# A graph-network layer on one Trainium2 core: x loaded ahead of most convolution taps, and the first message moved between the filter steps

## The chip, the cores and the metric

The kernel runs on one core of one Trainium2 chip. The core has TensorE (PE, matrix products), VectorE (DVE), ScalarE (ACT), GpSimd (POOL), SyncE (SP, used here for DMA issue alone) and 16 DMA engines that all queues share. The metric is the device time of one execution, in microseconds, lower being better. The kernel before takes 1842.6 us (median of 3 runs, 1842.21 to 1846.51). A difference of 0.3%, about 5.5 us, is what a measurement of this kernel can tell from none.

## The reference

64 graphs of 256 nodes with 256 channels. A layernorm and a relu give h; a graph layer of h is added to x.

```python
h = jnp.maximum(_layernorm(x, axis=-1), 0.0)
# the layer, with x standing for h, and mask for adj
xc = jnp.transpose(x, (0, 2, 1))
h = relu(_bn(_conv1d(xc, conv1_w, 0), bn1...))          # 1 tap
h = _bn(_conv1d(h, conv2_w, 8), bn2...)                 # 17 taps along the nodes
x_conv = jnp.transpose(jax.nn.relu(h + xc), (0, 2, 1))
s = x @ w_se.T + b_se                                   # 3 numbers a node
sq = jnp.sum(s * s, axis=-1)
dist = sq[:, :, None] + sq[:, None, :] - 2.0 * jnp.einsum('bnd,bmd->bnm', s, s)
A = jnp.exp(-dist) * mask
msg = jax.nn.relu(x @ w_msg.T + b_msg)
x_nmp = jnp.einsum('bnm,bmd->bnd', A, msg)
x_in = jnp.concatenate([x_conv, x_nmp], axis=-1)
gi = x_in @ w_ih.T + b_ih
gh = x @ w_hh.T + b_hh                                  # then the gates of a GRU cell
```

All in float32.

## The kernel before

The 64 graphs are worked in pairs (32 pairs, numbered i from 0), and eight graphs, four pairs, make a batch b. The convolution with 17 taps is done as a fast transform along the nodes: VectorE transforms conv1's output (`split_steps`, `fft.odd`, `fft.even`), TensorE multiplies each of 16 frequency bins with transformed weights (`products`, which reads tiles `wb`), and VectorE transforms back. The transformed weights are made by the kernel itself, once, at the start. That start is what the change rearranges; the 1740 us after it are the same in both kernels but for what had been done earlier.

**The filter steps.** The taps (`c2_wT`, 256 input channels x 17 taps x 256 output channels, 4.46 MB) are laid out as 19 groups g of 7 input channels: 7 x 17 = 119 rows of a tile `taps`, for each of two chunks dc of 128 input channels. A step `filters(m, g, eng)` multiplies the group with a constant matrix `points[m]` (three of them, m = 0, 1, 2, for bins 0 to 5, 6 to 11, 12 to 15), copies the result from PSUM to a tile `fo` on ScalarE (L716; six buffers, used in turn), and stores it to a DRAM tensor `filt[m]` by the queue `eng` (L717). There are 57 steps. The first 18 take the groups 0 to 5 with all three m, the other 39 go through the groups 6 to 18 for m = 0, then for m = 1, then for m = 2. Stores go to GpSimd's queue and SyncE's in turn. `load_kind` (L728) loads the tiles `wb` from `filt`, nine of them before the last 17 steps.

The taps are loaded in parts (`load_taps`): `PARTS[0]` is groups 0 to 2, `PARTS[1]` groups 3 to 5, `PARTS[2]` groups 6 to 17, each for chunk 0 and chunk 1, first the 112 rows that split evenly; `load_last_taps` loads the seven rows left over, for all groups, and `load_last_group` group 18. Chunk 0 comes by SyncE's queue, chunk 1 by ScalarE's.

**Beside the filter steps** the first four pairs are normalised and pass conv1, in program order between the steps. `norm(i)`: VectorE takes statistics of X (L559 to L564), GpSimd raises the variance to the power of -0.5 (`rstd`, L565), VectorE scales X (L571). `transpose_h(i)`: TensorE transposes X into PSUM (L521), VectorE (pair 0) or ScalarE copies it with a relu to `hT`. `conv1(i)`: TensorE multiplies with `w_c1`, VectorE or ScalarE applies bn1 to give `h1`; `split_steps(i)` on VectorE follows. X of pairs 0 and 1 lies in tiles x, of pair 2 in tile Sv, of pair 3 in tile PT. `columns("bn1")` is a small TensorE transpose of bn1's four vectors, and is the first instruction of TensorE.

**Order.** [...]each engine works its instructions in the order of the program, and a waiting instruction holds up what is behind it on its engine, or on its DMA queue. A small planner (`Pace`) places VectorE's transform steps among the other work by estimated times. Each DMA raises a semaphore when it lands. Those of SyncE and ScalarE share eight in turn, those of GpSimd have eight of their own, so the issue of a DMA waits until the eighth before it has landed.

After the steps come the batches: `message(i)` (messages and s of a pair), `embed(i)` (a transpose of s-based rows `z`), `affinity(i)` (distances, exp, times adj), and `products`, `aggregate` and `gates` among them.

```python
    filter_steps(2)
    transpose_h(0)
    norm(1)
    for j in range(PB):
        ...
        conv1(j)
        ...
        run(split_steps(j))
        filter_steps((4, 4, 2, 2)[j])
    forward()
    filter_steps(len(steps) - (NG - FIRST) - 4)
    ...
    filter_steps(len(steps))
```

Of the kernel before, what the change touches and what calls it, by code (L numbers as in the profile page):

```python
# [13 lines left out]
FP = mybir.dt.float32  # L14
U16 = mybir.dt.uint16
AF = mybir.ActivationFunctionType
# [285 lines left out]
def kernel(  # L302
# [26 lines left out]
    nc = tc.nc  # L329
# [112 lines left out]
    make_identity(nc, ident)  # L442
    neg_half = const.tile([P, G * MC], FP)
    nc.gpsimd.memset(neg_half, -0.5)

# [8 lines left out]
    def load_taps(dc, a, b, eng):  # L456
        v = c2_wT[dc * P + a * KG:dc * P + b * KG].rearrange("(g k) t o -> (k t) g o", k=KG)
        eng.dma_start(out=taps[:MAIN, a:b, dc, :], in_=v[:MAIN])
# [31 lines left out]
            eng.dma_start(out=t[a:a + n[j]], in_=v.rearrange("(k p) -> k p", p=P))  # L490
        ROWS[name] = t, n

    load_vectors("bn2", bn2 + [ih_b, hh_b], nc.gpsimd)
    load_points(0, nc.scalar)
    for dc, eng in ((0, nc.sync), (1, nc.scalar)):
        load_taps(dc, *PARTS[0], eng)
        load_last_taps(dc, eng)
    load_x(0)
    load_vectors("bn1", bn1, nc.scalar)
    w_c1 = const.tile([P, DC, D], FP)  # L500
    nc.scalar.dma_start(out=w_c1, in_=c1_wT.rearrange("(k p) o -> p k o", p=P))
    for n in range(1, len(PASSES)):
        load_points(n, nc.scalar)
    load_taps(0, *PARTS[1], nc.sync)
    load_x(1)
    load_taps(1, *PARTS[1], nc.scalar)
    load_taps(0, *PARTS[2], nc.sync)
    load_taps(1, *PARTS[2], nc.scalar)
    load_last_group(0, nc.sync)
    load_last_group(1, nc.scalar)  # L510
    load_x(2)
    load_x(3)

    pace = Pace()

# [71 lines left out]
        run(b)  # L587

    norm(0)
    def fold_bn(params, name, factor=1.0):  # L590
        g, b, m, v = params
        scale = const.tile([P, DC], FP, name=f"{name}_scale")
        shift = const.tile([P, DC], FP, name=f"{name}_shift")
        nc.vector.tensor_scalar(scale, v, BN_EPS, None, ALU.add)
        nc.gpsimd.tensor_tensor(scale, scale, neg_half[:, :DC], ALU.pow)
        nc.vector.tensor_mul(scale, scale, g)
        nc.vector.tensor_mul(shift, m, scale)
        nc.vector.tensor_sub(shift, b, shift)
        if factor != 1.0:
            nc.vector.tensor_scalar(scale, scale, factor, None, ALU.mult)  # L600
        return scale, shift

    bn1 = columns("bn1")
    nc.scalar.activation(const.tile([P, 1], FP, name="unused"), neg_half[:, :1], AF.Relu)
    s1, h1_shift = fold_bn(bn1, "bn1")


# [334 lines left out]
    steps = deque((m, g) for g in range(FIRST) for m in range(len(PASSES)))  # L942
    steps.extend((m, g) for m in range(len(PASSES)) for g in range(FIRST, NG))

    def filter_steps(n):
        for k in range(n):
            filters(*steps.popleft(), nc.gpsimd if len(steps) % 2 else nc.sync)

    filter_steps(2)
    transpose_h(0)  # L950
    norm(1)
    for j in range(PB):
        if j > 0:
            transpose_h(j)
        if 0 < j < PB - 1:
            norm(j + 1)
        if j == 2:

            w_msg = const.tile([P, DC, D + SE], FP)
            nc.gpsimd.dma_start(out=w_msg[:, :, D:], in_=se_wT.rearrange("(k p) s -> p k s", p=P))  # L960
            b_msg = const.tile([P, D + SE], FP)
            for t, v in ((b_msg[:, :D], msg_b), (b_msg[:, D:], se_b)):
                nc.gpsimd.dma_start(out=t, in_=bass.AP(tensor=v.tensor, offset=v.offset, ap=[[0, P], [1, v.shape[0]]]))
            nc.sync.dma_start(out=w_msg[:, :, :D], in_=msg_wT.rearrange("(k p) o -> p k o", p=P))
            load_adj(0, nc.sync)
        conv1(j)
        if j == 2:
            *bn2, b_ih, b_hh = columns("bn2")
            s2, h2_shift = fold_bn(bn2, "bn2", 1.0 / L)
            b_rz = const.tile([P, 2 * DC], FP)  # L970
            nc.vector.tensor_add(b_rz, b_ih[:, :2 * DC], b_hh[:, :2 * DC])
            nc.vector.tensor_scalar(b_rz, b_rz, 0.5, None, ALU.mult)
        run(split_steps(j))
        filter_steps((4, 4, 2, 2)[j])
    forward()
    filter_steps(len(steps) - (NG - FIRST) - 4)
    for n in range(3):
        for kind in range(3):
            load_kind(0, n, kind)
# [6 lines left out]
    for b in range(NB):  # L986
        i = b * PB
        nxt = i + PB
        message(i)
        pace.flush(odd)  # L990
        products(b, 0)
        embed(i)
        products(b, 1)
        pace.add(fft.branch_back(Yv, T, 0))
        affinity(i)
        if b > 0:
            load_adj(i + 1)
        products(b, 2)
        if b > 0:
            finish(i - 1)  # L1000
        else:
            transpose_a(i)
        products(b, 3)
        pace.flush(even)
        if b == 0:
            norm(nxt)
        else:
            run(norm_steps(nxt + 1)[0])
        pace.add(fft.branch_back(Yv, T, 2))
        pace.add(fft.odd_back(Yv, T))  # L1010
        aggregate(i)
        if b > 0:
            join_adj(i + 1)
        else:
            nc.gpsimd.dma_start(out=w_hh, in_=hh_wT.rearrange("(k p) o -> p k o", p=P))
            nc.gpsimd.dma_start(out=w_ih, in_=ih_wT.rearrange("(k p) o -> p k o", p=P))
        products(b, 4)
        message(i + 1)
        products(b, 5, lambda i=i: embed(i + 1))
        pace.add(mix(fft.q_back(Yu, T), fft.odd_factors(Yv)))  # L1020
        if b == 0:
            pace.add(norm_steps(nxt + 1)[0], normed[1])
        affinity(i + 1)
        if b > 0:
            load_adj(i + 2)
            join_h(nxt)
        products(b, 6)
        if b == 0:
            transpose_a(i + 1)
            transpose_h(nxt)  # L1030
        products(b, 7)
        pace.add(mix(fft.p_back(Yu, T), fft.q_factors(Yu)), scaled)

        def join(j):
            pace.add(fft.join(Yu, Yv, T, slice(2 * G * j, 2 * G * (j + 1))))
            pace.add([(W, lambda o=o: residual(i + j, o)) for o in range(DC)], joined[j])
        join(0)
        pace.add(norm_steps(nxt + 2)[0], normed[2])
        join(1)
        if b == 0:  # L1040
            turn_adj(3)
            keep_adj(3)
        aggregate(i + 1)
        if b > 0:
            join_adj(i + 2)
        message(i + 2)
        pace.flush(normed[1])
        turn_h(nxt + 1)

        def wait():  # L1050
            pace.flush(scaled)
            affinity(i + 2, True)
            conv1(nxt)
            pace.add(split_steps(nxt), halved)
            join(2)
            pace.flush(joined[0])
        gates(i, 0, wait, lambda i=i: embed(i + 2))
        if b == 0:
            transpose_a(i + 2)
            load_y(0)  # L1060
        load_adj(i + 3)
        sort_h(nxt + 1)
        turn_adj(nxt)
        keep_adj(nxt)

        def early():
            join_h(nxt + 1)
            pace.flush(normed[2])
            turn_h(nxt + 2)
        gates(i, 1, None, early)  # L1070
        pace.flush(halved)
        conv1(nxt + 1)
        join(3)
        pace.add(split_steps(nxt + 1), halved)
        pace.add(norm_steps(nxt + 3)[0], normed[3])
        aggregate(i + 2)
        join_adj(i + 3)
        pace.flush(joined[1])
        sort_h(nxt + 2)
        turn_adj(nxt + 1)  # L1080
        keep_adj(nxt + 1)
        gates(i + 1, 0, lambda nxt=nxt: join_h(nxt + 2))
        pace.flush(normed[3])
        turn_h(nxt + 3)
        pace.flush(halved)
        conv1(nxt + 2)
        pace.add(split_steps(nxt + 2), halved)
        pace.add(norm_steps(nxt + 4)[0], normed[0])
        finish(i)
        sort_h(nxt + 3)  # L1090
        turn_adj(nxt + 2)
        keep_adj(nxt + 2)
        gates(i + 1, 1)
        join_h(nxt + 3)
        message(i + 3)
        conv1(nxt + 3)
        pace.add(split_steps(nxt + 3), halved)
        if b + 1 < NB:
            forward()
        pace.flush(normed[0])  # L1100
        pace.flush(joined[2])

        def wait():
            affinity(i + 3)
            turn_h(nxt + 4)
        gates(i + 2, 0, wait, lambda i=i: embed(i + 3))
        sort_h(nxt + 4)
        turn_adj(nxt + 3)
        keep_adj(nxt + 3)
        aggregate(i + 3)  # L1110
        finish(i + 1)
        load_adj(nxt)
        gates(i + 2, 1)
        join_adj(nxt)
        pace.flush(joined[3])
        gates(i + 3, 0)
        finish(i + 2)
        gates(i + 3, 1)
# [46 lines left out]
```

## Time and profile before

| what | value |
|---|---|
| time | 1842.6 us, median of 3 |
| span of the profiled execution | 1841.8 us |
| TensorE busy | 1799.2 us (98%) |
| VectorE, ScalarE, GpSimd busy | 1366.2, 728.5, 220.5 us |
| first matmul | 13.84 us |
| last filter step ends, first message begins | about 103 us |
| first `products` begin | 106.62 us |
| DMA | 245.96 MB, mean 134 GB/s over the span |

A line of the profile's groups, waits or timeline names the engine, the line of the kernel, the operation, the tile written and the tiles read, and in brackets the time for which the engine had been idle, with what ended it. "PE" is a matmul, "PEld" the load of its weights, which runs beside matmuls. A float32 product of the program stands in the trace as two records, so a filter step is four and a conv1 of a pair is eight. The clock of TensorE in the records is a share of its full speed; it was 0.5 from 40.9 to 47.7 us. In lines of DMA issue the first two numbers are start and length of the issue, with the waits between issues of one group in it.

### The profile page before, as it was taken

What the parts mean: (1) busy time and instruction counts of PE and PEld (TensorE: products, weight loads), DVE (VectorE), ACT (ScalarE), POOL (GpSimd) and SP (SyncE); (2) the same over time, 40 slices, a digit from 0 to 9 for tenths busy, and PEclk for the clock granted to TensorE, in tenths of its full rate; (3) what the DMA queues carried; (4) which work ended last, traced back from release to release, by engine and by line L of the source; (5) the groups of instructions that cost most, each with busy time, mean ns of one, the idle gap of its engine ahead of it and who ended that gap; (6) DMA issues with size and microseconds to landing.
All of it is one profiled execution on the core that took longest, in us unless ns stands there. A gap on an engine that the chain in (4) does not pass through costs nothing.

```text
span 1841.8 us, 21877 instructions
## 1 busy us (share of the span) xinstructions
PE 1799.2 (98%) x7494; PEld 1113.6 (60%) x7494; DVE 1366.2 (74%) x2594; ACT 728.5 (40%) x1443; POOL 220.5 (12%) x359
## 2 busy tenths in 40 slices
PE   5999999999999999999999999999999999999997
PEld 3687454964569444784448645595546844487453
DVE  4879669795879849797697967888587974979422
ACT  2535532364323642255422653236432463224321
POOL 2210101100111011111012000110111110110000
PEclk9999999999999999999999999999999999999999
DMA  7777554854548444564347645384544744173011
GB/s 197 241 244 233 117 101 90 243 140 108 104 102 258 104 103 92 154 194 116 83 99 216 164 94 108 90 261 114 112 103 123 215 111 92 38 193 106 12 35 34
DMA packets 250498, 245.96 MB, mean 134 GB/s; under 512 B 143080, under 2 KB 176644, under 8 KB 250387
## 3 DMA queue, kind: packets, MB, share of 16 engines
q1 hardware_dynamic: 216362, 183.31, 36.9%
q0 software_dynamic: 31072, 58.60, 14.2%
q10 hardware_dynamic: 2953, 2.66, 0.7%
q8 instruction: 59, 0.97, 0.2%
q14 instruction: 52, 0.43, 0.1%
HBM read 156.56 MB, written 44.30 MB: 109 GB/s over the span
## 4 chain that ended last, share of the span: by engine, by line
PE 93%; issue 3%; DVE 2%; DMA 1%; POOL 1%; ACT 0%; ACTq 0%; POOLq 0%; DVEq 0%
PE acc L517 79%; PE aux L517 10%; PE aux L521 2%; PE aux L829 1%; POOL filt L717 1%; DMA taps<-in_c_wT_dram 1%; DMA points<-points 0%; DVE Yv L59 0%; DMA filt<-fo 0%; DVE T L65 0%; DVE Yv L62 0%; ACT e L830 0%; DVE msg L801 0%; DVE st L559 0%; POOL rstd L565 0%
## 5 line engine op out<-in xcount | busy, mean ns | idle before, releaser
L517 PE MATMUL acc<-xnm,w_ih 128*128 128x512 f32 x768 | 353.1, 592 | 0.0
L517 PE MATMUL acc<-hT,w_hh 128*128 128x512 f32 x768 | 350.5, 592 | 0.0
L517 PE MATMUL acc<-Yv,w_ih 128*128 128x512 f32 x768 | 342.7, 596 | 1.1 <-ACT Yv L789 1.1
L517 PEld LDWEIGHTS acc<-Yv,w_ih 128*128 128x128 f32 x768 | 145.8, 191 | 184.6 <-issue 180.9
L517 PEld LDWEIGHTS acc<-xnm,w_ih 128*128 128x128 f32 x768 | 144.7, 190 | 176.0 <-issue 174.4
L517 PEld LDWEIGHTS acc<-hT,w_hh 128*128 128x128 f32 x768 | 143.9, 190 | 164.6 <-issue 155.0
L891 DVE SCALAR_TENSOR_TENSOR gn<-tr,gn 128x512 f32<-128x512 f32 x64 | 44.1, 689 | 209.4 <-ACT tr L889 209.3
L889 ACT ACTIVATE tr<-acc,b_rz 128x512 f32<-128x512 f32 x64 | 44.0, 687 | 362.7 <-PE acc L517 362.7
L917 POOL DMA_DIRECT2D out_dram<-y x64 | 39.4, 620 | 797.6 <-DVE y L916 772.4
L517 PE MATMUL acc<-V,wb 128*128 128x128 f32 x1024 | 124.8, 275 | 0.0
L517 PE MATMUL acc<-U,wb 128*128 128x128 f32 x1024 | 124.3, 276 | 0.0
L517 PEld LDWEIGHTS acc<-U,wb 128*128 128x128 f32 x1024 | 120.4, 192 | 3.6 <-DVE T L59 2.0
L59 DVE SCALAR_TENSOR_TENSOR V<-T,V 128x256 f32<-128x256 f32 (+2 forms) x224 | 121.5, 607 | 0.3
L517 PE MATMUL acc<-hT,w_c 128*128 128x512 f32 x256 | 119.1, 609 | 1.3 <-ACT hT L633 1.3
L517 PEld LDWEIGHTS acc<-V,wb 128*128 128x128 f32 x1024 | 119.5, 192 | 0.0
L517 PE MATMUL aux<-e,msg 128*128 128x256 f32 x464 | 104.9, 379 | 0.0
L517 PEld LDWEIGHTS aux<-e,msg 128*128 128x128 f32 x464 | 87.1, 190 | 17.7 <-issue 6.9
L565 POOL TENSOR_TENSOR rstd<-rstd,neg_half 128x4 f32<-128x4 f32 x32 | 37.5, 1170 | 473.7 <-DVE shift L567 343.1
L896 ACT ACTIVATE nn<-gn,bn_columns 128x512 f32<-128x512 f32 x64 | 46.2, 722 | 115.7 <-DVE gn L894 115.7
L517 PE MATMUL aux<-w_msg,hT 128*128 128x259 f32 x384 | 89.6, 382 | 0.0
L517 PEld LDWEIGHTS acc<-hT,w_c 128*128 128x128 f32 x256 | 48.2, 194 | 60.2 <-issue 53.0
L426 ACT COPY adj<-adjh 128x1024 uint16<-128x1024 uint16 x58 | 73.9, 1344 | 23.3 <-DMA adjh<-halves_d 23.3
(160 smaller groups left out, 2715.7 us busy)
## 6 DMA issues: line engine op xcount, KB each, us to landing
wb<-filt SPq DMA_DIRECT2D x376, 256.0 KB
y<-in_x_dram POOLq DMA_DIRECT2D x64, 256.0 KB, 5.8
out_dram<-y POOLq DMA_DIRECT2D x64, 256.0 KB, 5.7
x<-in_x_dram SPq DMA_DIRECT2D x60, 256.0 KB
halves_d<-halves SPq DMA_DIRECT2D x116, 128.0 KB
adjh<-halves_d POOLq DMA_DIRECT2D x116, 128.0 KB, 6.2
hh<-halves SPq DMA_DIRECT2D x108, 128.0 KB
filt<-fo POOLq DMA_DIRECT2D x18, 252.0 KB, 5.4
```

The lines of the kernel that those rows point to most:

```text
L59: return self.step(out, lambda: self.v.scalar_tensor_tensor(out, x, s, y, op0=ALU.mult, op1=ALU.add))
L426: nc.scalar.copy(v[:, j], u[:, j])
L517: nc.tensor.matmul(p, w, v, **kw)
L521: nc.tensor.transpose(p, v, ident)
L565: nc.gpsimd.tensor_tensor(t["rstd"], t["rstd"], neg_half, ALU.pow)
L717: eng.dma_start(out=filt[m][g * KG:g * KG + size].rearrange("k t c o -> (k t) (c o)"), in_=t[:size * kinds])
L829: nc.tensor.matmul(p[:, :N], ZT[rows_q, :P], ZT[rows_q, P:], start=True, stop=True)
L889: nc.scalar.activation(tr, pr, AF.Tanh, bias=b_rz[:, dc:dc + 1], scale=0.5)
L891: nc.vector.scalar_tensor_tensor(gn, tr, 1.0, gn, op0=ALU.add, op1=ALU.mult)
L896: nc.scalar.activation(nn, gn, AF.Tanh, bias=b_ih[:, 2 * DC + dc:2 * DC + dc + 1])
L917: nc.gpsimd.dma_start(out=rows(out, G * i + g), in_=row_tile(Y[i], g))
```

## The change

The order of the loads at the start is new, as are the queues that carry them, and a piece of the first batch's work moves forward:

- ScalarE's table load and a first dummy activation come first on ScalarE; then it issues the three `points`, bn1's vectors and `w_c1`, and no taps.
- On SyncE, x of pair 0 comes first, then chunk 0 of the first taps, x of pair 1, taps of part 1, x of pairs 2 and 3, and then the large part 2.
- Chunk 1 of the taps comes by GpSimd's queue: part 0 at the start, part 1 after `norm(0)`, part 2 after `norm(1)`. The six vectors of bn2 and the gates come after `norm(1)`, instead of first.
- The first 18 filter steps are all done beside the first four pairs (3 + 4 + 4 + 3 + 4 instead of 2 + 4 + 4 + 2 + 2), and their stores all go to GpSimd's queue; after them the two queues take turns as before.
- `message(0)`, `embed(0)` and `affinity(0)`, with the load of the second adj that follows it, stand between the filter steps instead of after them.

The aim is that x and the points don't wait for taps, that ScalarE is free early, and that stores of the filter steps get some slack.

```diff
+    nc.scalar.activation(const.tile([P, 1], FP, name="unused"), neg_half[:, :1], AF.Relu)
...
-    load_vectors("bn2", bn2 + [ih_b, hh_b], nc.gpsimd)
-    load_points(0, nc.scalar)
-    for dc, eng in ((0, nc.sync), (1, nc.scalar)):
-        load_taps(dc, *PARTS[0], eng)
-        load_last_taps(dc, eng)
-    load_x(0)
+    for n in range(len(PASSES)):
+        load_points(n, nc.scalar)
     load_vectors("bn1", bn1, nc.scalar)
     w_c1 = const.tile([P, DC, D], FP)
     nc.scalar.dma_start(out=w_c1, in_=c1_wT.rearrange("(k p) o -> p k o", p=P))
-    for n in range(1, len(PASSES)):
-        load_points(n, nc.scalar)
+    load_x(0)
+    for dc, eng in ((0, nc.sync), (1, nc.gpsimd)):
+        load_taps(dc, *PARTS[0], eng)
+        load_last_taps(dc, eng)
+    load_x(1)
     load_taps(0, *PARTS[1], nc.sync)
-    load_x(1)
-    load_taps(1, *PARTS[1], nc.scalar)
-    load_taps(0, *PARTS[2], nc.sync)
-    load_taps(1, *PARTS[2], nc.scalar)
-    load_last_group(0, nc.sync)
-    load_last_group(1, nc.scalar)
     load_x(2)
     load_x(3)
+    load_taps(0, *PARTS[2], nc.sync)
+    load_last_group(0, nc.sync)
...
     norm(0)
+    load_taps(1, *PARTS[1], nc.gpsimd)
...
-            filters(*steps.popleft(), nc.gpsimd if len(steps) % 2 else nc.sync)
+            filters(*steps.popleft(), nc.sync if k_done[0] >= 18 and len(steps) % 2 else nc.gpsimd)
+            k_done[0] += 1
...
-    filter_steps(2)
+    filter_steps(3)
     transpose_h(0)
     norm(1)
+    load_vectors("bn2", bn2 + [ih_b, hh_b], nc.gpsimd)
+    load_taps(1, *PARTS[2], nc.gpsimd)
+    load_last_group(1, nc.gpsimd)
...
-        filter_steps((4, 4, 2, 2)[j])
+        filter_steps((4, 4, 3, 4)[j])
     forward()
-    filter_steps(len(steps) - (NG - FIRST) - 4)
+    n = len(steps) - (NG - FIRST) - 4
+    filter_steps(n // 2)
+    message(0)
+    filter_steps(4)
+    embed(0)
+    filter_steps(2)
+    affinity(0)
+    filter_steps(n - n // 2 - 6)
...
-        message(i)
+        if b > 0:
+            message(i)
         pace.flush(odd)
         products(b, 0)
-        embed(i)
+        if b > 0:
+            embed(i)
         products(b, 1)
         pace.add(fft.branch_back(Yv, T, 0))
-        affinity(i)
         if b > 0:
+            affinity(i)
             load_adj(i + 1)
```

More of the change, by code (lines that the diff above doesn't have):

```diff
@@ L603 @@
     bn1 = columns("bn1")
-    nc.scalar.activation(const.tile([P, 1], FP, name="unused"), neg_half[:, :1], AF.Relu)
     s1, h1_shift = fold_bn(bn1, "bn1")
@@ L943 @@
     steps.extend((m, g) for m in range(len(PASSES)) for g in range(FIRST, NG))
+    k_done = [0]
     def filter_steps(n):
         for k in range(n):
-            filters(*steps.popleft(), nc.gpsimd if len(steps) % 2 else nc.sync)
-    filter_steps(2)
+            filters(*steps.popleft(), nc.sync if k_done[0] >= 18 and len(steps) % 2 else nc.gpsimd)
+            k_done[0] += 1
+    filter_steps(3)
     transpose_h(0)
     norm(1)
+    load_vectors("bn2", bn2 + [ih_b, hh_b], nc.gpsimd)
+    load_taps(1, *PARTS[2], nc.gpsimd)
+    load_last_group(1, nc.gpsimd)
     for j in range(PB):
```

## The prediction

> **What bounds the kernel now.** I read the page first, then the TensorE instructions in order of time, then the windows of the first 37 us, then the queue of SyncE. The page's busy shares and slices:
>
> ```profile
> PE 1799.2 (98%) x7494; PEld 1113.6 (60%) x7494; DVE 1366.2 (74%) x2594; ACT 728.5 (40%) x1443; POOL 220.5 (12%) x359
> ...
> PE   5999999999999999999999999999999999999997
> ```
>
> TensorE bounds the kernel: 98% busy, and of 42.6 us without a matmul most lies in the first slices. The change touches only what runs before the first `products`, so all it can win is TensorE idle time, and cold-clock time, ahead of that point. TensorE in order of time (start, us, instruction, idle before it):
>
> ```profile
> 13.84 0.24 PE L538 MATMUL aux<-ident,bn_rows 8*128 8x8 f32 x1 [13.84 <-DMA bn_rows<-in_bn_v_dram]
> 14.01 2.07 PE L517 MATMUL acc<-taps,points 119*126 119x256 f32 x4
> 18.57 2.07 PE L517 MATMUL acc<-taps,points 119*126 119x256 f32 x4 [2.49 <-DMA points<-points]
> ...
> 34.90 3.62 PE L517 MATMUL acc<-taps,points 119*126 119x256 f32 x16
> 41.01 2.30 PE L521 MATMUL aux<-ident,Sv 128*128 128x128 f32 x8 [2.49 <-DVE Sv L571]
> 44.04 5.53 PE L517 MATMUL acc<-hT,w_c 128*128 128x512 f32 x8 [0.73 <-ACT hT L633]
> ...
> 52.82 3.70 PE L517 MATMUL acc<-hT,w_c 128*128 128x512 f32 x8 [0.29 <-ACT hT L633]
> ```
> ```profile
> 88.63 1.95 PE L517 MATMUL acc<-taps,points 119*77 119x256 f32 x8 [0.44 <-ACT fo L716]
> 91.67 1.09 PE L517 MATMUL acc<-taps,points 119*77 119x256 f32 x4 [1.09 <-ACT fo L716]
> 94.30 1.95 PE L517 MATMUL acc<-taps,points 119*77 119x256 f32 x8 [1.54 <-ACT fo L716]
> 97.89 1.99 PE L517 MATMUL acc<-taps,points 119*77 119x256 f32 x8 [1.64 <-ACT fo L716]
> 101.02 2.06 PE L517 MATMUL acc<-taps,points 119*77 119x256 f32 x8 [1.14 <-ACT fo L716]
> ```
>
> Idle: 13.84 before the first matmul; 2.49 for the second block of points; 2.49 for graph pair 2 (tile Sv); 0.26 + 0.73 + 0.29 for hT; 5.85 in the last nine filter steps. Sum 25.95. A filter step (4 records) takes 0.90 warm (16 records in 3.62) and 2.07 cold; a conv1 pair takes 3.70 warm, 5.53 after the idle stretch at 38.5. So the idle 2.49 at Sv costs about 5.5 in all. Why loads come late, from the windows (columns: length, then busy times, clock, DMA share, GB/s):
>
> ```profile
> 5.00:11.00 6.00, 0.00 (x0) 0.00 (x0) 0.00 (x0) 0.00 (x0) 0.00 (x0) 1.00 0.61 111
> 11.00:20.00 9.00, 3.68 (x8) 2.52 (x9) 3.58 (x15) 1.17 (x1) 1.61 (x2) 1.00 0.99 211
> 20.00:27.00 7.00, 7.00 (x20) 3.97 (x19) 3.02 (x9) 1.28 (x4) 2.20 (x6) 1.00 1.11 251
> ```
>
> Once the DMA engines are full they move 211 to 251 GB/s of taps (rows of 1 KB), and 4.46 MB of taps + 2.1 MB of x need near 30 us: the order of the loads decides. And SyncE's queue:
>
> ```profile
> 83.11 6.73 SPq L728 DMA_DIRECT2D wb<-filt  x9
> 92.67 11.51 SPq L717 DMA_DIRECT2D filt<-fo  x9
> ```
>
> The nine wb loads hold SyncE's queue until 92.67; stores of fo behind them are late, six fo buffers are used up, and TensorE has the 5.85.
>
> **What the Trainium skill says.** (1) "TensorE: Matmul & The Clock Gate", Part 1, "What's actually happening": TensorE falls to half its clock after an idle window of about 3.4 us and comes back after one of work. The trace agrees: 5.53 against 3.70 for the same conv1. (2) "DMA: Bandwidth & Descriptors", "Issuing engines are not separate DMA queues": SyncE, ScalarE and GpSimd queues share the same 16 engines. The trace agrees: DMA share 0.99 to 1.11 with two queues at work, so moving loads to GpSimd adds no capacity. (3) Same page, "SWDGE vs HWDGE vs iDMA": engines take turns between GpSimd's descriptors and the others', by packets of up to 4096 B. In the trace's DMA queues between 136 and 144 us, GpSimd's queue, loading w_ih, held 71.0% and moved 2.23 MB against SyncE's 0.86. That share I use below.
>
> **Part by part.**
>
> ScalarE's table load (1.28) and its dummy activation (0.20) move ahead of its loads; points leave from 2.2 instead of 0.74. Nothing needs them before 13. ScalarE no longer issues taps, so it is free for fo copies at about 11 rather than 18.8.
>
> Start. DMAs of SyncE and ScalarE share eight semaphores in turn, so each waits for the eighth before it. In the new order bn1's last two vectors wait for the seven leftover tap rows of SyncE. Those landed at about 8.1 before (then bn_rows went out, and landed at 13.84); x (0.52 MB, about 2 us at 251 GB/s) is now ahead of them, so they land near 10.5; bn_v then has no taps ahead in ScalarE's queue: 2 to 2.5 us instead of 5.7. First matmul at 13.0 (11.5 to 14.5), a gain of 0.8. x of pair 0 lands by 6 and its norm is done near 10, off the path. GpSimd's two tap loads cost its engine 0.7 each (as its other loads: 0.53 to 0.80), before anything waits for it.
>
> Then TensorE, in its new order: bn 0.2, filters 2.07 + 2.07 + 1.0 (all points there; the wait of 2.49 is gone): 18.3. Transposes 1.1, hT 0.8, conv1 3.5: 23.7. Four steps 3.6: 27.3. Transposes 1.1, hT 0.3, conv1 3.5, four steps 3.6: 35.8. Transposes of Sv 1.1: 36.9. Pair 2 is loaded before the large taps now, and its norm is done by about 34 (DVE: norm 1 to 24.9, evacuation and split 5.0, norm 2 4.5), so the wait for Sv is gone as well.
>
> What takes its place: conv1 of pair 2 needs hT from ScalarE, and ScalarE stands in order behind the copies into fo of steps 10 and 11, which reuse the buffers of steps 4 and 5. The stores of these are on GpSimd now, behind six bn2 vectors (6 x 0.52) and the large taps part of chunk 1 (1.38 MB). GpSimd gets there after rstd of norm 1 (23.3): 23.3 + 3.3 = 26.6, issue about 27.5. I take 300 GB/s in all, between the 251 of taps alone and the 388 of 136 to 144 us. With 67% of it (near the 71% above) the taps land at 27.5 + 6.9 = 34.4, the two stores (0.25 MB each, 1.25 each) at 37.0. With half the bandwidth: 9.2 + 3.0, near 39.5. I take 37: conv1 at 37.0 + copy 0.6 + hT 0.8 = 38.4, idle about 1.5, less than the 2.49 that dropped the clock. Conv1 3.7: 42.1; bn2 + three steps 2.9; transposes 1.1; 0.3 + 3.5; four steps 3.6: 53.5. Eighteen steps are then done. Before, twelve were done at 56.35 and six more (0.89 each) made 61.7. Gain 8.2.
>
> Rest: 39 steps, message (103.01 to 106.62: 3.6), embed and affinity (about 1.0): same TensorE work, only in another order, so no gain by itself. The nine wb loads still stand 17 steps before the end, and still block SyncE; I expect the same 5.85. Message and affinity let stores catch up by 4.6, but give ScalarE about the same in small work (z, zT, exp), so I count nothing. The second adj (0.5 MB) moves into GpSimd's queue among the stores, where it waits for VectorE's e (4 x 0.60): stores behind it are late by 1 to 2. I take 1 lost. VectorE stays hidden: its odd transform (59.85 to 84.2, 24.4) starts near 54 and ends before the filters do. Sum: 8.2 - 1.0 = 7.2; 1842.6 - 7.2 = 1835.4.
>
> **Rivals.**
>
> Cold wait behind the taps (chance 0.22). GpSimd's queue gets half the bandwidth, stores land at 39.5, conv1 starts at 40.8, the clock has dropped, conv1 takes 5.5: eighteen steps at 57.5, gain 4.2 - 1.0. For: SyncE has x 4, w_msg and adj (1.3 MB) queued in the same stretch. Against: the 71% share. 1839.4.
>
> Given back at the wb loads (0.13). adj and nine wb loads (2.8 MB) fall together with the stores, on two queues, and the 5.85 grows by 5 to 7. For: this is where TensorE runs out of buffers today. Against: 274 to 400 GB/s flow there. About 1841.
>
> GpSimd's queue becomes the bound (0.15), the other side. All of the first 18 stores, the taps, bn2 and every rstd stand in one order; queued behind a waiting store are rstd of norms 2 and 3, and behind these VectorE and TensorE. The trace shows no GpSimd load of 1344 rows; by its rows (0.53 for 126, 0.80 for 512) issue is 1 to 2 us, but should it be 6 or more, or should small bn2 loads land after 9 (the 9.4 of the start) and again hold the stores, TensorE waits twice more, cold each time: 3 x 4 us lost against about 5.5 gained, about 1849.
>
> **How the numbers follow.** Forecast 0.50, rivals 0.22, 0.13, 0.15. Faster by over 0.3% means under 1837.1: the forecast, and a quarter of the first rival, 0.55. The third rival beyond 1848.1 and its tail: 0.13. Between: 0.32. The range begins where TensorE starts at 11.5 and never waits at pair 2 (1.2 + 1.5 more, and 2 to 3 of the 5.85 saved): 1829.5. It ends at 1846, past the second rival; what lies above is less than 2 in 10 with what lies below.
>
> **What would show it.** Right: first matmul at 11.5 to 14.5; no idle before the second filter step; idle before conv1 of pair 2 under 2.5, released by hT, while ScalarE's copy before it waits for a store of filt on GpSimd's queue; clock full from about 18 to the end; first `products` near 100 instead of 106.6; idle of 5 to 8 in the last 17 steps. Wrong: clock at half near 40; GpSimd's rstd waiting behind stores by several us; x or taps of chunk 1 landing later than 11 at the start; a stall longer than 8 around the wb loads; or a difference that arises after the first `products`.

## The result and the profile after

| | before | changed |
|---|---|---|
| time, median | 1842.43 us (1842.21 to 1846.51) | 1850.66 us (1848.73 to 1854.01) |
| ratio to before | | 1.0043, 95% interval 1.0025 to 1.0062 |
| span of the profiled execution | 1841.8 us | 1852.2 us |
| first matmul | 13.84 us | 21.85 us |
| first `products` | 106.62 us | 118.04 us |

The changed kernel is slower by 8.2 us, and lies above the range that was given. The page of the changed kernel, its busy times and the slices of TensorE with the clock:

```profile
PE 1801.4 (97%) x7494; PEld 1115.2 (60%) x7494; DVE 1365.6 (74%) x2594; ACT 729.9 (39%) x1443; POOL 230.0 (12%) x374
...
PE   4889999999999999999999999999999999999997
...
PEclk9889999999999999999999999999999999999999
```

TensorE idles for 1852.2 - 1801.4 = 50.8 us, 8.2 more than before (1841.8 - 1799.2 = 42.6), and is busy for 2.2 more with the same number of matmuls, because more of them run at half clock. The sum, 10.4, is the whole difference of the spans. The first three slices (46 us each) hold it: each is less full than it was, and the granted clock falls in slices two and three. Nothing is lost later: the first `products` come 11.4 later, of which about 1.0 is `embed` and `affinity`, now done ahead of them, and what follows takes 1734.2 us instead of 1735.2. The profiled execution is the slowest of the four (1854.01; the others took 1852.33, 1848.99 and 1848.73), so what its trace shows need not all be in the others. TensorE of the changed kernel in order of time (start, us, instruction, idle before it and what ended it):

```profile
21.85 0.24 PE L535 MATMUL aux<-ident,bn_rows 8*128 8x8 f32 x1 [21.85 <-DMA PT<-in_x_dram]
22.02 5.11 PE L514 MATMUL acc<-taps,points 119*126 119x256 f32 x12
...
43.72 1.04 PE L518 MATMUL aux<-ident,Sv 128*128 128x128 f32 x8
53.02 5.82 PE L514 MATMUL acc<-hT,w_c 128*128 128x512 f32 x8 [8.27 <-ACT hT L631]
...
104.02 3.09 PE L514 MATMUL acc<-taps,points 119*77 119x256 f32 x12 [1.55 <-ACT fo L714]
107.84 1.09 PE L514 MATMUL acc<-taps,points 119*77 119x256 f32 x4 [0.73 <-ACT fo L714]
109.98 1.09 PE L514 MATMUL acc<-taps,points 119*77 119x256 f32 x4 [1.05 <-ACT fo L714]
112.59 5.52 PE L514 MATMUL acc<-taps,points 119*77 119x256 f32 x12 [1.52 <-ACT fo L714]
118.04 2.08 PE L514 MATMUL acc<-Sv,wb 128*128 128x128 f32 x8
```

Three places. TensorE begins 8.0 later. Three filter steps then run without a gap and the transposes of Sv no longer wait: both waits of 2.49 are gone, as intended. But before conv1 of pair 2 there is a new wait of 8.27, and after it the clock is down (5.82 for a conv1 that takes 3.70 at full clock). And ahead of the first `products` the clock falls again, to 0.5 from 111.9 to 122.2 us: twelve records take 5.52, where twelve took 3.09 just before.

Who held the start is seen in ScalarE's DMA issues:

```profile
13.92 0.25 ACTq L491 DMA_DIRECT2D bn_rows<-in_bn_b_dram  x1
16.51 0.24 ACTq L491 DMA_DIRECT2D bn_rows<-in_bn_m_dram  x1
16.79 0.27 ACTq L491 DMA_DIRECT2D bn_rows<-in_bn_v_dram  x1
```

and in the program's list of instructions, which names the semaphore that each waits for. SyncE's and ScalarE's transfers use eight in turn: number 2 is raised by chunk 0's main taps rows, 3 by its seven leftover rows, 5 by `points1`.

```
bn_rows<-in_bn_b_dram  [waits DMAHW2]
bn_rows<-in_bn_m_dram  [waits DMAHW3]
bn_rows<-in_bn_v_dram  [waits DMAHW5]
```

So bn_b went out when the main rows had landed, bn_m when the leftover rows had (16.5), bn_v right behind it, and bn_v was in use 5.06 after its issue (21.85 - 16.79). The releaser that the TensorE line names, a load of PT, only happened to land at that time: e3, e4 and e8 (below) begin at 20.86 to 22.31 too, and name bn_v.

Who held conv1 of pair 2 is seen on GpSimd and on ScalarE, which copies filter results (`fo`) ahead of hT:

```profile
34.99 1.14 POOL L459 DMA_DIRECT2D taps<-in_c_wT_dram  x1
36.12 0.52 POOL L467 DMA_DIRECT2D taps<-in_c_wT_dram  x1
37.90 0.54 POOL L715 DMA_DIRECT2D filt<-fo  x1 [1.25 <-DMA bn_rows<-in_bn_g_dram]
```
```profile
50.95 0.58 ACT L714 COPY fo<-acc 126x512 f32<-126x512 f32 x1 [8.13 <-DMA filt<-fo]
```

The copy of step 10 needs the buffer of step 4, whose store was issued on GpSimd's queue behind 1.4 MB of taps, and came free 16.0 after these had been issued (50.95 - 34.99). hT stands behind two such copies in ScalarE's order, and runs at 52.37, though TensorE had transposed Sv by 44.76.

### The profile page after: what moved, and what is told of

Its sections match the earlier page's. It is cut to its first block, busy times and chain, and to the rows that moved or that the text cites. A ratio compares the mean times of both kernels' runs of the same rounds, so it can differ in the third digit from the quotient of the medians.

```text
span 1852.2 us, 21876 instructions
## 1 busy us (share of the span) xinstructions
PE 1801.4 (97%) x7494; PEld 1115.2 (60%) x7494; DVE 1365.6 (74%) x2594; ACT 729.9 (39%) x1443; POOL 230.0 (12%) x374
## 4 chain that ended last, share of the span: by engine, by line
PE 95%; DMA 2%; DVE 1%; issue 1%; ACT 0%; POOL 0%; SPq 0%; POOLq 0%; ACTq 0%; DVEq 0%
PE acc L514 81%; PE aux L514 10%; PE aux L518 2%; PE aux L827 1%; DMA x<-in_x_dram 1%; DMA filt<-fo 1%; DMA bn_rows<-in_bn_b_dram 0%; ACT e L828 0%; DVE Yv L59 0%; POOL filt L715 0%; DVE T L65 0%; DVE Yv L62 0%; DVE e L834 0%; SPq L377 0%; DVE msg L799 0%
## 5 line engine op out<-in xcount | busy, mean ns | idle before, releaser
L514 PEld LDWEIGHTS aux<-w_msg,hT 128*128 128x128 f32 x384 | 72.2, 190 | 17.2 <-issue 7.2
```

The source lines that it names most:

```text
L514: nc.tensor.matmul(p, w, v, **kw)
```

## The experiments

Each undoes or moves one thing in the changed kernel; the later ones combine. In the table "idle" is TensorE's before conv1 of pair 2, and the ratio is to the kernel before, run beside it on the same chip. The before's median was 1842.8 beside e1 to e4, 1843.5 beside e5 to e8 and 1843.7 beside e9 to e11, so differences of about 1 us between the groups mean nothing. Medians are over 4 to 20 executions. First matmul, idle and first `products` come from one profiled execution, which can lie some us off the median (e1's 3.9 below, the changed kernel's 3.4 above).

| run | median us | ratio, 95% interval | first matmul | idle | first `products` |
|---|---|---|---|---|---|
| changed | 1850.66 | 1.0043 (1.0025 to 1.0062) | 21.85 | 8.27 | 118.04 |
| e1 taps ahead of x(0) | 1844.93 | 1.0010 (0.9999 to 1.0020) | 16.91 | 6.93 | 107.44 |
| e2 bn1 later | 1846.92 | 1.0018 (1.0011 to 1.0025) | 17.09 | 5.92 | 112.28 |
| e3 big taps on SyncE | 1839.47 | 0.9978 (0.9970 to 0.9986) | 21.79 | 0.34 | 104.21 |
| e4 message back | 1849.90 | 1.0033 (1.0022 to 1.0045) | 20.86 | 7.87 | 116.50 |
| e5 = e3 + e1 | 1835.88 | 0.9961 (0.9948 to 0.9973) | 17.71 | 0.34 | 100.83 |
| e6 = e3 + e1 + e2 | 1833.74 | 0.9951 (0.9935 to 0.9966) | 7.68, then 12.17 | 0.34 | 99.42 |
| e7 = e3, first taps by SyncE and ScalarE | 1852.89 | 1.0049 (1.0032 to 1.0067) | 31.56 | 0.34 | 115.52 |
| e8 stores on SyncE | 1837.82 | 0.9975 (0.9962 to 0.9988) | 22.31 | 0.34 | 104.03 |
| e9 bn1 on GpSimd's queue | 1844.84 | 1.0005 (0.9995 to 1.0014) | 14.51 | 8.91 | 109.92 |
| e10 = e5 + bn1 on GpSimd's queue | 1833.32 | 0.9944 (0.9924 to 0.9964) | 13.77 | 1.32 | 99.14 |
| e11 = e8 + e1 + e2 | 1835.80 | 0.9958 (0.9945 to 0.9970) | 7.83, then 13.10 | 0.44 | 103.06 |

### The wait of 8.27: e3 and e8

e3 moves the big taps of chunk 1 to SyncE's queue, and leaves the stores on GpSimd's:

```diff
     load_taps(0, *PARTS[2], nc.sync)
     load_last_group(0, nc.sync)
+    load_taps(1, *PARTS[2], nc.sync)
+    load_last_group(1, nc.sync)
...
-    load_taps(1, *PARTS[2], nc.gpsimd)
-    load_last_group(1, nc.gpsimd)
```

> The large part of chunk 1 of the taps and its group 18 go on SyncE's queue, behind those of chunk 0, instead of GpSimd's; all else as in the changed kernel. Theory (ScalarE waits 8.13 for stores that stand behind these taps in GpSimd's queue): stores of steps 4 and 5 land within 8 us of their issue, idle before conv1 of pair 2 is under 2.5 instead of 8.27, no half clock near 50, time 7 to 10 us below the changed kernel. Rival (the DMA engines as a whole are the limit there): the wait moves to the stores or to taps behind x and stays over 5, time within 3 us of the changed kernel.

e8 does the opposite: the taps stay on GpSimd's queue, and the stores of steps 4 to 18 leave it.

```diff
-            filters(*steps.popleft(), nc.sync if k_done[0] >= 18 and len(steps) % 2 else nc.gpsimd)
+            filters(*steps.popleft(), nc.sync if 3 <= k_done[0] < 18 or k_done[0] >= 18 and len(steps) % 2 else nc.gpsimd)
```

> The changed kernel with the stores of filter steps 4 to 18 on SyncE's queue, the big taps still on GpSimd's. If the 8.3 us before the second pair's conv1 come from the order within GpSimd's queue (the small stores stand behind 1.4 MB of taps), that idle time falls under 2.5 us and the time by 6 to 10: 1841 to 1845. If they come from the bandwidth that the taps take at that time from everything, the idle time stays above 5 and the time within 3 of the changed kernel: 1848 to 1852. First matmul unchanged at 20.9 to 21.9 either way.

e3 came out 11.2 and e8 12.8 below the changed kernel, though both begin as late as it does. Both won more than was expected (7 to 10, and 6 to 10). TensorE at conv1 of pair 2 in e3, then in e8 with the transposes before it, then e8's first `products`:

```profile
44.39 3.70 PE L516 MATMUL acc<-hT,w_c 128*128 128x512 f32 x8 [0.34 <-ACT hT L633]
```
```profile
43.59 1.04 PE L518 MATMUL aux<-ident,Sv 128*128 128x128 f32 x8
44.98 3.70 PE L514 MATMUL acc<-hT,w_c 128*128 128x512 f32 x8 [0.34 <-ACT hT L631]
```
```profile
104.03 1.16 PE L514 MATMUL acc<-Sv,wb 128*128 128x128 f32 x8
```

The wait is gone and conv1 is at full clock: it ends at 48.1 in e3 and 48.7 in e8 instead of 58.8, which is most of what they win. The `products` begin 13.8 and 14.0 earlier; the rest of that arises in the last filter steps. Was it the DMA engines' capacity? The DMA views of the same 35 to 51 us, first of the changed kernel, then of e8 (queue 0 is GpSimd's, 1 SyncE's: packets, MB, share of the 16 engines; then issues with KB each and us from issue to landing):

```profile
DMA packets 1660, 3.85 MB, mean 240 GB/s; under 512 B 267, under 2 KB 446, under 8 KB 1659
...
q0 software_dynamic: 842, 2.43, 52.2%
q1 hardware_dynamic: 817, 1.41, 32.0%
...
taps<-in_c_wT_dram POOLq DMA_DIRECT2D x1, 1344.0 KB, 14.6
filt<-fo POOLq DMA_DIRECT2D x4, 252.0 KB, 12.9
```
```profile
DMA packets 2013, 4.03 MB, mean 252 GB/s; under 512 B 272, under 2 KB 535, under 8 KB 2011
...
q1 hardware_dynamic: 1497, 2.54, 47.3%
q0 software_dynamic: 514, 1.46, 31.1%
...
taps<-in_c_wT_dram POOLq DMA_DIRECT2D x1, 1344.0 KB, 9.6
```

No: all in all 3.85 MB moved in one and 4.03 in the other. What differs is that large loads and small stores which somebody waits for shared one queue. Shown, then: the wait comes from their being on the same queue, from either side (in e3 the stores, still on GpSimd's queue, land 6.0 after issue at the median, instead of 12.9). The stores did not stand strictly behind the taps. The taps landed 14.6 after their issue, at 49.6, and from 35 to 49.6 us GpSimd's queue moved 2.25 MB. The taps are 1.41 MB of that (1378 KB), so about 0.84 MB were stores, served among the taps. Taps and stores delayed each other: the taps took 14.6 instead of e8's 9.6. Why the first store was through only at 50.95, after the taps, is not shown.

### The start: e1, e2, e7, e9

e1 puts SyncE's first taps ahead of x of pair 0:

```diff
-    load_x(0)
     for dc, eng in ((0, nc.sync), (1, nc.gpsimd)):
         load_taps(dc, *PARTS[0], eng)
         load_last_taps(dc, eng)
+    load_x(0)
     load_x(1)
```

> One part undone: on SyncE's queue chunk 0 of the first taps (with its leftover rows) goes ahead of x of pair 0 again, all else as in the changed kernel. Theory (x ahead of the taps delays them, the leftover rows start late and bn1's last vectors wait for them): leftover rows land near 9 instead of 16.5, first matmul at 13 to 15 instead of 21.85, time 5 to 8 us below the changed kernel, about 1843. Rival (it is GpSimd's queue that takes the DMA engines from SyncE's small rows, whatever stands first): first matmul stays at 20 or later, time within 2 us of the changed kernel.

e2 takes bn1's transposes and fold from TensorE's head, behind the first three filter steps:

```diff
-    bn1 = columns("bn1")
-    s1, h1_shift = fold_bn(bn1, "bn1")
...
     filter_steps(3)
+    bn1 = columns("bn1")
+    s1, h1_shift = fold_bn(bn1, "bn1")
     transpose_h(0)
```

> The transpose of bn1's vectors and the few instructions after it move behind the first three filter steps, the loads stay as they are. Theory (TensorE waits for the last bn1 vector, 5 us behind the leftover rows): the first filter step starts at 17 to 18, when the leftover rows have landed, the transpose of bn1 comes without a wait near 22, and the time is 3 to 5 us below the changed kernel. Rival (taps of chunk 1 by GpSimd's queue land later still, so bn1 hides nothing): first filter step at 20 to 22, time within 1.5 us of the changed kernel.

In e1 the leftover rows landed by 7.2 instead of 16.5: the last load of x in the group below waits for their semaphore, and its issue began at 7.17.

```profile
1.65 6.11 SPq L377 DMA_DIRECT2D x<-in_x_dram  x4
```
```profile
11.69 0.25 ACTq L491 DMA_DIRECT2D bn_rows<-in_bn_b_dram  x1
```

So x ahead of them had cost 9.3, and the rival is out: GpSimd's queue had the same first taps to load. But the turn of the semaphores now put bn_b behind x of pair 0 (number 2), which landed at 11.7. bn_v went out at 12.28 and the first matmul ran at 16.91, 4.6 after that: later than the 13 to 15 expected, and 5.7 less time. In e2 the first filter step ran at 17.09, just when the leftover rows had landed (bn_m, which waits for them, went out at 17.02), 4.9 ahead of the changed kernel's (22.02). A part was lost again to hT, which waited 2.27 for the later fold, and to the conv1 behind it (5.29 instead of 3.70); the wait before pair 2 was shorter in turn (5.92), and 3.7 remained, as expected. So two things make the start of the changed kernel: the leftover rows at 16.5, because x is ahead of them, and then bn_v's 5 us.

e7 was to tell whether GpSimd's queue, which carries chunk 1's first taps, slows SyncE's. It puts these back where the kernel before had them, on top of e3:

```diff
-    for n in range(len(PASSES)):
-        load_points(n, nc.scalar)
+    load_points(0, nc.scalar)
+    for dc, eng in ((0, nc.sync), (1, nc.scalar)):
+        load_taps(dc, *PARTS[0], eng)
+        load_last_taps(dc, eng)
+    load_points(1, nc.scalar)
+    load_points(2, nc.scalar)
     load_vectors("bn1", bn1, nc.scalar)
...
-    for dc, eng in ((0, nc.sync), (1, nc.gpsimd)):
-        load_taps(dc, *PARTS[0], eng)
-        load_last_taps(dc, eng)
```

> As e3, but the first taps and leftover rows stand where they stood in the kernel before: chunk 0's on SyncE ahead of x(0), chunk 1's on ScalarE's queue behind the first points and ahead of bn1. Nothing of the start is on GpSimd's queue. If GpSimd's queue is what keeps the start at 16.9 in e1 and at 21.8 in the changed kernel, the first matmul comes at 13 to 15 (13.8 in the kernel before) and the time is 7 to 8 below e3: 1831 to 1833. If it is only the x rows ahead on SyncE, the start is e1's 16.9 and the time e5's, about 1834.

Neither: the first matmul came at 31.56, and the time is 13.4 above e3's. ScalarE's issues in e7:

```profile
13.58 3.69 ACTq L481 DMA_DIRECT2D points<-points  x2
17.92 0.28 ACTq L491 DMA_DIRECT2D bn_rows<-in_bn_g_dram  x1
20.91 0.27 ACTq L491 DMA_DIRECT2D bn_rows<-in_bn_b_dram  x1
22.91 0.24 ACTq L491 DMA_DIRECT2D bn_rows<-in_bn_m_dram  x1
26.18 0.24 ACTq L491 DMA_DIRECT2D bn_rows<-in_bn_v_dram  x1
```

`points1` and `points2` and all four vectors now wait for semaphores (7, 0 and 1 to 4 in turn) of transfers ahead of them, each issue for another landing (bn_v for a load of PT, x of pair 3), where three points and a vector of the changed kernel were out by 6.3. A further 2.63 went on `w_c` ahead of the first conv1. The two queues are one chain in this respect, and putting two more large loads ahead of the vectors made each of them wait. So e7 leaves its own question unanswered; the 7.2 of e1 answers it for the leftover rows.

e9 therefore takes only the vectors out of that chain: in the changed kernel the four bn1 vectors go to GpSimd's queue, behind chunk 1's first taps. GpSimd's transfers have eight semaphores of their own, so nothing is waited for there. (The turn of what stays shifts too: `w_c` goes out at 5.57 instead of 17.10.)

```diff
-    load_vectors("bn1", bn1, nc.scalar)
...
         load_last_taps(dc, eng)
+    load_vectors("bn1", bn1, nc.gpsimd)
     load_x(1)
```

> The changed kernel with one move: the four bn1 vectors go on GpSimd's queue, right behind chunk 1's first taps. In the changed kernel's instruction list the HW transfers of SyncE and ScalarE share eight completion semaphores in turn: bn_b waits for the one of chunk 0's main taps rows, bn_m for that of the leftover rows, bn_v for points1's; GpSimd's transfers have eight of their own, of which the first taps use two, so there the vectors wait for nothing. If the late start is these waits (issue only after the leftover rows land, then 5 us to land), the vectors are issued by 5.5 and landed by 15, the first step starts when the leftover rows land, 15 to 17.5, and the time falls by 4 to 6: 1845 to 1847. If it is bandwidth alone (the same bytes in the same 20 us), the first matmul stays above 20 and the time within 2: 1849 to 1852.

```profile
14.51 0.24 PE L535 MATMUL aux<-ident,bn_rows 8*128 8x8 f32 x1 [14.51 <-DMA bn_rows<-in_bn_v_dram]
15.66 5.46 PE L514 MATMUL acc<-taps,points 119*126 119x256 f32 x12 [0.91 <-DMA taps<-in_c_wT_dram]
```

The first filter step begins at 15.66 instead of 22.02, when the leftover rows land, and conv1 of pair 0 at 22.46 instead of 28.35: 5.9 earlier, and the time is 5.8 less. The wait before conv1 of pair 2 stays (8.91). The theory of the waits holds. The rows themselves landed hardly sooner: the transfers that wait for the main and the leftover rows went out at 14.16 and 15.59 (13.92 and 16.51 in the changed kernel), with no fewer bytes moving (185 GB/s over the first 25 us, 161 in the changed kernel). The vectors, issued by 5.2, were there by 14.51.

### The message: e4

e4 puts `message(0)`, `embed(0)` and `affinity(0)` back behind all filter steps.

> The first message, embedding and affinity go back behind the filter steps, all else as in the changed kernel. Theory (this move wins nothing, and the adj load among the stores costs 1 to 2): time 0 to 3 us below the changed kernel, with idle of 5 to 7 in the last 17 steps. Rival (the move is what let the stores catch up and earns 3 or more): time 3 us or more above the changed kernel, with more idle in the last 17 steps.

0.8 less, within the intervals of the two ratios: the move neither wins nor loses anything that these runs can tell. The idle time of the last steps was 3.89, less than the 5 to 7 expected.

### Together: e5, e6, e10, e11

e5 is e3 with e1's edit, e6 is e5 with e2's edit, e10 is e5 with e9's edit (the vectors behind both of GpSimd's first taps loads), e11 is e8 with e1's and e2's edits.

> The two single edits together: chunk 1's part 2 taps and group 18 on SyncE's queue (alone 11.2 us off the changed kernel), and SyncE's first taps and leftover rows ahead of x(0) (alone 5.7 off). Theory that these are two separate losses, a late start and a wait behind the big taps in GpSimd's queue: first matmul at 16.9, no idle of more than 1 us before the second pair's conv1, about 1834 (1832 to 1836). Rival, that both edits relieve one and the same loss, for instance stores and loads that have to be through before the product stage: the second adds nothing to the first, 1838 to 1840, with the idle time moved to the last filter steps.

> As e5, and bn1's transposes and fold behind the first three filter steps. If TensorE then waits only for the first taps and leftover rows (issued first on SyncE, landed near 12 with x behind them; chunk 1's on GpSimd's queue), the first matmul is a filter step at 12 to 14 and the time 3 to 5 below e5's: about 1830. If the rows of chunk 1 on GpSimd's queue hold it, the first step stays at 16 to 17 and the time is e5's within 1. If the later fold holds hT, as alone in e2 (2.3 of idle), half of the gain comes back: 1832 to 1833.

> e5 (big taps on SyncE, first taps ahead of x(0)) with the bn1 vectors on GpSimd's queue behind chunk 1's first taps. By the semaphore theory no vector waits for a taps transfer; vectors and leftover rows of both chunks have landed by 12 to 14.5, first matmul then (e5: 17.7), no idle before any conv1 over 1 us, time 3 to 5 below e5: 1831 to 1833, the equal of e6 without its wait for hT or a little better. If bandwidth sets the start, 16 to 18 and 1835 to 1837.

> e8 (stores of steps 4 to 18 on SyncE, big taps left on GpSimd's queue) with e1's and e2's edits. If the order within GpSimd's queue and the start are the only two losses, this is e6's equal: first filter step at 12 to 13, idle before the second pair's conv1 under 1 us, 1831 to 1835. If the big taps on GpSimd's queue cost something else too, apart from the stores (e8 came out 1.7 below e3, so nothing speaks for it yet), 1837 or more.

The two losses are separate and nearly add: 11.2 for e3 and 5.7 for e1 alone, 14.8 for both. e6 and e10 are within their intervals of each other, and at 0.9951 and 0.9944 both beat the kernel before. e6 came out by its third case, 0.7 above the range given for it: 2.1 below e5, with the wait for hT (2.37); its first two records ran as early as 7.68, and the rest of the step when the taps were there, at 12.17. e10 is 0.3 above its range, its vectors in time at 13.77 and its idle before conv1 of pair 2 at 1.32, a little over the 1 that was allowed. e11 lies 0.8 above its range and below the 1837 of its second case, with an interval that meets e6's. Its trace is of the slowest of its eight executions and shows the clock down in the last steps (twelve records in 5.52). So no further cost of the big taps on GpSimd's queue is shown, and none is ruled out. e10, page and TensorE's start:

```profile
PE 1795.6 (98%) x7494; PEld 1111.9 (61%) x7494; DVE 1366.2 (75%) x2594; ACT 730.5 (40%) x1443; POOL 230.2 (13%) x376
...
PEclk9999999999999999999999999999999999999999
```
```profile
13.77 0.24 PE L537 MATMUL aux<-ident,bn_rows 8*128 8x8 f32 x1 [13.77 <-DMA bn_rows<-in_bn_v_dram]
13.94 5.49 PE L516 MATMUL acc<-taps,points 119*126 119x256 f32 x12
```

It begins when the kernel before does (13.84), keeps what the change set out to win, and never falls to half clock after its start: idle 1831.8 - 1795.6 = 36.2, 6.4 less than before, and busy for 3.6 less.

## Why the prediction was wrong

- **What bounds it.** Right: TensorE, and the whole difference arises ahead of the first `products`.
- **The start, "first matmul at 13.0": failed**, by 8.9. The waits were named as they are; two terms were too small. "Near 10.5" for the leftover rows was 16.5, and "2 to 2.5" for bn_v was 5.1. The first took 8.1 of the kernel before and added about 2 for x, by 251 GB/s; e1 puts the cost of x ahead at 9.3. That rate was read later, at 20 to 27 us, with mostly taps in flight; the prediction's own table has 111 GB/s for 5 to 11 us. The DMA view of the changed kernel from 8 to 17 us shows what there was:

```profile
DMA packets 929, 1.23 MB, mean 137 GB/s; under 512 B 170, under 2 KB 657, under 8 KB 929
...
q1 hardware_dynamic: 704, 0.89, 56.9%
q0 software_dynamic: 113, 0.31, 19.3%
q10 hardware_dynamic: 112, 0.04, 2.6%
```

  That is 0.14 MB a us, with the engines occupied for 79% of the time. For the second the trace of before already had 5.7, and taps ahead were put down as its cause; without them it was 5.1. The Trainium skill, "DMA: Bandwidth & Descriptors", "Queues, rings and completion order", says that a transfer's semaphore is raised only after every earlier write of the same DMA engine, across its queues. The 5.1 for 1 KB agrees with that, though no run separates it from other causes.
- **TensorE from its first matmul to the transposes of Sv.** Right: 23.9 forecast, 22.9 measured (44.76 - 21.85), and both waits of 2.49 gone.
- **The wait before conv1 of pair 2, "idle about 1.5": failed**, and this costs as much as the start: 6.8 (8.27 - 1.5), and 2.1 for the clock. The wait, its engine and its buffers were named; the taps' issue came 13.1 after the first matmul (14.5 forecast). Two things about the transfer were wrong. The rate: GpSimd's queue was to move 201 GB/s, 67% of 300. From 35 to 49.6 us it moved 2.25 of 3.57 MB, 154 GB/s. The share, 63%, was nearly right; the total was 244 GB/s, not 300. At 154 GB/s the taps would take 9.2 instead of 6.9, near the 9.6 of e8. And the order: the stores were put behind the taps, 2.6 after them. In fact 0.84 MB of stores were served among the taps; the taps landed after 14.6, and the first store was through 16.0 after the taps' issue, not 9.5. The rival "cold wait" had the same mechanism, with stores at 12 after issue, and was too small as well.
- **The sum of these.** To the end of the eighteenth step: 8.9 - 1.0 + 6.8 + 2.1 = 16.8. Measured are about 16.6: 70.1 (66.52 and four steps of 0.89) against 53.5. By the prediction's count the kernel before is there at 61.7, so the changed one has lost 8.4 by then. The last steps add about 2 in this trace.
- **The rest, "I count nothing" and "I take 1 lost".** The first fits e4, which shows no difference. For the second the issue of adj waited 2.0 for VectorE, and the idle time of the last steps was 4.85, against 5.85 forecast for them, so the rival "given back at the wb loads" did not come true. What was not foreseen there is the second fall of the clock, from 111.9 to 122.2 us. Two slips of the working changed nothing: the points left at 1.41, not 2.2, and a start at 11.5 is 1.5 ahead of 13.0, not 1.2.
- **The rival on the other side, "about 1849".** The time was near it by luck: more than half of the forecast's miss to the eighteenth step is the late start, which this rival does not have. Of its mechanism one part came true, GpSimd's queue as the bound: TensorE waited once behind it, where this rival counted three such waits, while the issue of the large taps took 1.1, not 6, and the small bn2 loads held stores for 1.25 and 0.56.

## What to carry to other kernels

Look for small transfers that an engine waits for on one queue with a large one that nobody waits for yet: here two kernels that separated them, each in its own way, were rid of 8 us of waiting with about the same bytes in flight. Where a program's transfers share completion semaphores in turn, the order of issue alone makes small loads wait for large ones: read the list of waits, put in the landing time of each as measured at that stage, and see whether the vectors can go by a queue whose semaphores are free. And a change that is right in its aim can lose by its new order: here three small edits (e3, e1 and e9, together e10) turned 8.2 us of loss into 10.3 of gain.

## What the hardware showed that was not expected

- The clock fell before the first `products` of the changed kernel after waits of 1.55, 0.73, 1.05 and 1.52 us with work between them. The Trainium skill, "TensorE: Matmul & The Clock Gate", Part 1, "What's actually happening", gives one idle window of about 3.4 us as the condition; no single wait here was that long. Nor was the 2.49 after which the kernel before was at half clock from 40.9 to 47.7: the prediction's "the trace agrees" holds for the half clock, not for the length of the wait. In e3 waits of 1.77, 1.66, 0.82 and 0.57 in the same steps left the clock full, and in e5 one of 2.03; in e11 it fell after 0.20, 1.44 and 0.76. It fell in these steps in seven traces (the changed kernel, e2, e4, e6, e7, e8, e11) and stayed full in the other six. What decides between the two stays open.
- The large taps load on GpSimd's queue took 14.6 us with stores issued behind it on its queue, 9.6 without them, at nearly the same total of bytes on all queues (3.85 and 4.03 MB in 16 us).
